# Graph network on one Trainium2 core: the edge keys and weight parts of strips 2 to 24 turned by a DMA transpose through DRAM

## The chip, the cores and the metric

The kernel runs on 1 core of one Trainium2 chip. The metric is the device time of one execution in microseconds (us). The kernel before took 1860.86 us, the median of three runs (1860.08 to 1861.27).

The names used below: PE is the engine for matrix products, PEld its weight loads, DVE the vector engine, ACT the scalar engine, POOL the general engine, and SP the engine that here does nothing but issue DMAs. Each engine works through its own instructions in order and waits only on semaphores. "SPq" and "POOLq" are rows of the sequencer.

## The reference

Four graph layers act in turn on a table `x` of 6250 nodes with 128 features. Each one normalises `x`, gathers neighbours over the 206250 edges (which are sorted by `dst`), sums them per node and adds the result to `x`.

```python
h = jnp.maximum(_layernorm(x, axis=-1), 0.0)
msg = edge_weight[:, None] * h[src]                       # layer 0
neighbor = jax.ops.segment_sum(msg, dst, num_segments=6250)
out = neighbor @ W1.T + b1 + (h * neighbor) @ W2.T + b2
x = x + jax.nn.leaky_relu(out, negative_slope=0.2)
...
agg = jax.ops.segment_sum(h[src], dst, num_segments=6250)  # layer 1, then by degree, gelu, graph norm
...
summed = jax.ops.segment_sum(x_clique[min(dst, 3124)], src, num_segments=6250)  # layer 2, mean over edges
...
agg = jax.ops.segment_sum(m[src], dst, num_segments=6250)  # layer 3, GRU gates
```

No gather is done row by row. The kernel first builds, for every strip of 256 destination nodes, a dense matrix of edge counts (for layers 1 to 3) and a dense matrix of edge weights (for layer 0), and the sums over edges become dense products.

## The kernel before

`fast` has two stages. In the first, which ends at about 1018 us of the profile, 25 strips are worked through one after another. `strip(k, nb)` covers 2 blocks of 128 nodes (the last strip one block). In the second stage, layers 1 to 3 run as dense products over the counts (`dense`, L1088) to the end. The change lies in the first stage alone.

**A strip.** It takes 8 pieces, and a piece 4 calls of `count`. A call makes 24 small products on PE (L781) of one-hot matrices, `s_hot` for the low 7 bits of the source and `k_hot` for its block, the latter times 1 and times three bf16 parts of the weight. ACT takes the result out of PSUM in two copies per call (L788 into `edge_w`, L790 into `cnt`). After every second call, `next(before)` issues a share of layer 0 of the strip before (L818, pairs of products that use one half of the array each). The one-hot matrices are made on DVE by `one_hots`, three instructions a piece (L759, L761, L762), one piece ahead: the pool `hot` has two buffers of each, so the matrices for piece p+1 can be written only when PE has finished piece p-1. The matrices for piece 0 of the next strip are made at the start of piece 7, from `following`, the pair of tiles that `prepare` hands out.

**What one-hots are made from.** `prepare(k)` is a generator that runs a strip ahead. It finds where the edges of 128 node pairs (one in each partition) begin, fetches 64 edges for each of the two nodes from the sorted lists with indirect DMAs on POOL (`fetch`, L639: `dst`, `src` and `wgt` for each half), and computes `vals`, five bf16 matrices of 128 pairs by 128 edges: two keys (L727, L730, on DVE) and three parts of the weight (`split`, L584 to L587, on POOL). The one-hots need these with edges along the partitions. So the last step turns them: five transposes on PE into one PSUM tile `pv` (L736), of the pool that the counts take their three buffers from too, and two copies on ACT into `keys` and `by_edge` (L741).

**The order.** It is written out by hand (`manual_schedule`), so an engine's instructions stand in the order in which Python issues them. `strip` calls `next(edges)` once at the middle of each piece named in `EDGES_AT` (in strip 0 at the start of the pieces in `FIRST_AT`), and a new `prepare(k + 2)` is begun at the end of piece 6 (`NEXT_AT`; in strip 0 after the last of `FIRST_AT`). In strips from 1 on the five steps are:

| step | piece | what `prepare` issues |
|---|---|---|
| begin | end of 6 | `junk` (L670, 1.9 us on DVE), fetch of `line` |
| 1 | 0 | `off` of half 0, fetch of `dst` half 0 |
| 2 | 2 | `off` of half 1, fetches `dst` half 1, `src` and `wgt` half 0 |
| 3 | 3 | fetches `src` and `wgt` half 1 |
| 4 | 5 | `vals`: keys on DVE, parts on POOL |
| 5 | 6 | five PE transposes, two ACT copies |

**What else the SP queue carries in a strip.** Two stores of finished counts (`cnt_d`, L969, 800 KB each, at the ends of pieces 3 and 7). Up to six steps of `turn` (`TURN_AT`: ends of pieces 1, 2, 3, 5, 6, 7), each a DMA transpose of 128 by 640 two-byte counts (`tt`, L801) and a store of the one before (L803); the 125 of them are through at about 895 us. From `finish0`, which ends the strip before, come a load of `xs` (piece 0), stores of `h_d` and `u_d` (L866, L867, piece 4) and a store of `f_d` (L880, piece 7). The add for `u_d` (L865) is on POOL.

Of the kernel before, what the change touches and what calls it, by code (L numbers as in the profile page):

```python
# [11 lines left out]
BF16 = mybir.dt.bfloat16  # L12
# [4 lines left out]
P = 128  # L17
# [454 lines left out]
TI = 2  # L472
# [22 lines left out]
U8, U16 = mybir.dt.uint8, mybir.dt.uint16  # L495
# [4 lines left out]
def fast(ctx: ExitStack, tc: tile.TileContext, a: dict, out: bass.AP, flag: bass.AP):  # L500


    nc = tc.nc
    const = ctx.enter_context(tc.tile_pool(name="f_const", bufs=1))
    dram = ctx.enter_context(tc.tile_pool(name="f_dram", bufs=1, space=bass.MemoryType.DRAM))
# [4 lines left out]
    identh = const.tile([P, P], BF16, name="f_identh")  # L510
# [23 lines left out]
    f_d = dram.tile([P, NB, D], F32, name="f_d")  # L534
    h_d = dram.tile([P, NB, D], F32, name="h_d")
    x_d = dram.tile([P, NB, D], F32, name="x_d")
    smp_d = dram.tile([NSMP, 1], I32, name="smp_d")

    def rows(table, g, nb):
# [42 lines left out]
    def split(eng, parts, src, rest):  # L582

        eng.tensor_copy(parts[0], src)  # L584
        eng.tensor_tensor(rest, src, parts[0], op=ALU.subtract)
        eng.tensor_copy(parts[1], rest)
        eng.tensor_tensor(parts[2], rest, parts[1], op=ALU.subtract)  # L587
# [9 lines left out]
    with ExitStack() as bx:  # L597
        def pool(name, bufs):
            return bx.enter_context(tc.tile_pool(name="b_" + name, bufs=bufs))
# [4 lines left out]
        banks = bx.enter_context(tc.tile_pool(name="b_banks", bufs=3, space=bass.MemoryType.PSUM))  # L604
# [28 lines left out]
        pay, hot = pool("pay", 2), pool("hot", 2)  # L633
# [4 lines left out]
        def fetch(t, name, idx):  # L638
            nc.gpsimd.indirect_dma_start(out=t, out_offset=None, in_=col[name],  # L639
                                         in_offset=bass.IndirectOffsetOnAxis(ap=idx, axis=0))  # L640
# [23 lines left out]
        def prepare(k):  # L664

            n0 = node0[:, k : k + 1]
            if k:
                junk = once.tile([P, NSMP], BF16, name="junk")
                r = small.tile([P, 1], F32, name="r")
                nc.vector.tensor_scalar(junk, smp, n0, None, op0=ALU.is_lt, op1=ALU.add, accum_out=r)  # L670
                at = small.tile([P, 1], F32, name="at")
                nc.vector.tensor_scalar(at, r, 1.0, 0.0, op0=ALU.subtract, op1=ALU.max)
                nc.vector.tensor_scalar(at, at, float(P), float(E - P), op0=ALU.mult, op1=ALU.min)
                at_i = small.tile([P, 1], I32, name="at_i")
                nc.vector.tensor_copy(at_i, at)  # L675
                line = once.tile([P, P], I32, name="line")
                fetch(line, "dst", at_i)
                yield
                less = once.tile([P, P], BF16, name="less")
                nc.vector.tensor_scalar(less, line, n0, None, op0=ALU.is_lt)  # L680
                c = small.tile([P, 1], F32, name="c")
                nc.vector.tensor_reduce(c, less, axis=mybir.AxisListType.X, op=ALU.add)
                off = small.tile([P, 1], F32, name="off")
                nc.vector.tensor_add(off, at, c)
            else:
                off = first_offsets()

            dst = once.tile([P, P], I32, name="dst")
            src = once.tile([P, P], I32, name="src")
            wgt = once.tile([P, P], F32, name="wgt")  # L690
            vals = pay.tile([P, 5, P], BF16, name="vals")
            same = once.tile([P, P], BF16, name="same")
            other = once.tile([P, P], BF16, name="other")
            halves_of = [(h, slice(h * H, (h + 1) * H)) for h in range(WN)]
            offs, nodes = [], []
            for h, half in halves_of:
                off_i = small.tile([P, 1], I32, name="off_i")
                nc.vector.tensor_scalar(off_i, off, float(E - H), None, op0=ALU.min)
                fetch(dst[:, half], "dst", off_i)
                offs.append(off_i)  # L700
                node = small.tile([P, 1], F32, name="node")
                nc.vector.tensor_scalar(node, n0, float(h), None, op0=ALU.add)  # L702
                nodes.append(node)
                if h + 1 == WN:
                    break
                if not k:
                    fetch(src[:, half], "src", off_i)
                    fetch(wgt[:, half], "edge_weight", off_i)
                yield
                here = deg[:, k, h : h + 1]  # L710
                nc.vector.tensor_scalar(same[:, half], dst[:, half], node, None, op0=ALU.is_equal,
                                        op1=ALU.add, accum_out=here)
                nc.vector.tensor_add(off, off, here)
            for (h, half), off_i in list(zip(halves_of, offs))[0 if k else 1 :]:
                fetch(src[:, half], "src", off_i)
                fetch(wgt[:, half], "edge_weight", off_i)
                yield
            one = nc.vector.tensor_scalar(same[:, half], dst[:, half], node, None, op0=ALU.is_equal,
                                          op1=ALU.add, accum_out=deg[:, k, WN - 1 : WN])
            if not k:  # L720
                first_same.append(one)
            for (h, half), node in zip(halves_of, nodes):
                nc.vector.tensor_scalar(other[:, half], dst[:, half], node, float(2 * P),
                                        op0=ALU.not_equal, op1=ALU.mult)
            sb = once.tile([P, P], I32, name="sb")
            nc.vector.tensor_scalar(sb, src, 7, None, op0=ALU.arith_shift_right)
            nc.vector.tensor_tensor(vals[:, 1, :], other, sb, op=ALU.add)  # L727
            sl = once.tile([P, P], I32, name="sl")
            nc.vector.tensor_scalar(sl, src, P - 1, None, op0=ALU.bitwise_and)
            nc.vector.tensor_copy(vals[:, 0, :], sl)  # L730
            rest = once.tile([P, P], F32, name="rest")
            split(nc.gpsimd, [vals[:, i, :] for i in (2, 3, 4)], wgt, rest)
            yield
            pv = banks.tile([P, 5, P], BF16, name="pv", tag="pK")
            for i in range(5):
                nc.tensor.transpose(pv[:, i, :], vals[:, i, :], identh)  # L736
            keys = pay.tile([P, P // TI, 2, TI], BF16, name="keys")
            parts = pay.tile([P, P // TI, 3, TI], BF16, name="by_edge")
            for t, i in ((keys, 0), (parts, 2)):
                to = pv[:, i : i + t.shape[2], :].rearrange("p i (q t) -> p q i t", t=TI)  # L740
                nc.scalar.copy(t, to)  # L741
            by_edge = keys, parts
            yield by_edge

        tq = TW // TI
# [148 lines left out]
        def normed(n):  # L894
            for _ in range(2 * n):
                next(norming)

        first = prepare(0)
        next(first)
        normed(4)  # L900
# [25 lines left out]
        by_edge = next(first)  # L926
        next(norming)
        hots = one_hots(by_edge, 0)
        before, ends, turns, edges = iter(()), [], turn(), prepare(1)


        END_AT, EDGES_AT, NEXT_AT = (0, 1, 2, 3, 4, 5, 7), (0, 2, 3, 5, 6), 6
        NORMS_AT = (0, 1, 3, 5), (0, 1, 2, 3)
        FIRST_AT = (2, 3, 4, 5, 6, 7)
        LAST_AT = (0, 2, 4, 6, 7, 10, 13)
        TURN_AT = (1, 2, 3, 5, 6, 7)

        def strip(k, nb):
# [4 lines left out]
            for w0 in range(0, last, PW):  # L943
                if w0 % TW == 0:
                    if k < 2 and piece in NORMS_AT[k]:
                        next(norming, None)
                    if not k and piece in FIRST_AT:
                        following = next(edges, None)
# [21 lines left out]
                if w1 % (PW * PT) and w1 < last:  # L970
                    continue
                if piece == (NEXT_AT if k else FIRST_AT[-1]) and k + 2 < NS:
                    edges = prepare(k + 2)
                    next(edges)
# [553 lines left out]
def gnn_kernel(tc: tile.TileContext, a: dict, out: bass.AP):  # L1528
    nc = tc.nc
    with tc.tile_pool(name="flag", bufs=1) as keep:  # L1530
        flag = keep.tile([1, 1], I32, name="flag")
        fast(tc, a, out, flag)
        found = nc.values_load(flag[0:1, 0:1], min_val=0, max_val=2 * E,
                               skip_runtime_bounds_check_because="a count of edges, each at most twice")
        with tc.If(found != E):
            general(tc, a, out)
# [48 lines left out]
```

## Time and profile before

| quantity | value |
|---|---|
| median of three runs | 1860.86 us |
| the profiled execution, as timed | 1859.0 us |
| its span, first to last instruction | 1857.2 us |
| first count of strip 0, on PE | 24.7 us |
| strip 0, from its first count to the next strip's | 41.4 us |
| strip 1 | 46.6 us |
| strips 2 to 23, together | 859.1 us |
| the shortest strip among them (23) | 38.63 us |
| the longest among them (3) | 41.60 us |
| first count of strip 24 | 971.7 us |

The lengths of strips are the distances between the first L781 product of one strip and of the next in the timeline. How to read the profile's lines: the page's first part gives each engine's busy time and share of the span. The 40 slices show busy tenths over time; one slice is 46.4 us, so the first stage is the first 22 slices. In a group of instructions, "a<-b" says which tile is written from which. "busy" counts overlapping instructions once. "mean" is the duration of one; on PE, where products overlap, it is far more than the distance from one to the next. A number in square brackets in a timeline is the idle time of that engine just before, with what ended it; "issue" there means that the profile shows nothing that was waited for.

Where the engines stand in the first stage, from the groups of instructions:

```profile
L741 ACT COPY by_edge<-pv 128x384 bf16<-128x384 bf16 x25 | 12.2, 490 | 0.0
L741 ACT COPY keys<-pv 128x256 bf16<-128x256 bf16 x25 | 9.4, 377 | 16.4 <-PE pv L736 16.4
L736 PE MATMUL pv<-f_identh,vals 128*128 128x128 bf16 x125 | 12.4, 227 | 14.6 <-DVE vals L730 12.5 <-POOL vals L584 1.3 <-POOL vals L586 0.6
```

These are the instructions that the change touches: 25 groups of five transposes and 25 pairs of copies. Of the 14.6 us that PE waited, 12.5 are one wait, at the very start of the kernel.

### The profile page before, as it was taken

The page shows a single profiled execution, that of the slowest core. Times are in us where ns is not written, and L with a number is a line of the kernel's source. Part 1 is how long each engine was busy: PE and PEld are TensorE (multiplying, and loading weights), DVE is VectorE, ACT ScalarE, POOL GpSimd, SP SyncE. Part 2 cuts the span into 40 slices and gives each one's busy share as a digit, 9 for nine tenths or more (in the row PEclk, how much of TensorE's full clock was granted, in tenths as well). Part 3 has the DMA queues.
Part 4 walks back from the last instruction along what each step waited for, and adds up shares of the span by engine and source line. Part 5 has one row for each costly group of instructions (what it writes and reads, how often), then busy time and mean ns, then how long its engine had stood idle before and what let it go on. Part 6 is the DMA issues. An engine that isn't in the chain of part 4 may idle for free. (4 is left out here: it accounts for less than half of the span.)

```text
span 1857.2 us, 65339 instructions
## 1 busy us (share of the span) xinstructions
PE 1791.2 (96%) x28191; PEld 1521.2 (82%) x28191; DVE 1381.6 (74%) x2946; ACT 1208.7 (65%) x2835; POOL 471.6 (25%) x431
## 2 busy tenths in 40 slices
PE   2799999999999999999999999999999999999997
PEld 2688888888888888888888888888888877787776
DVE  7878888888888888888886777777787755454444
ACT  6777777777777777777774677777565654443443
POOL 2333333433334333334332111111122210000000
PEclk9899999999999999999999999999999999999999
DMA  4245454644644544545223555554555444344342
GB/s 106 58 123 115 101 139 106 129 126 100 136 106 118 122 103 126 117 99 132 72 79 117 179 173 162 167 154 124 143 155 147 139 148 142 121 136 148 121 140 60
DMA packets 262513, 231.72 MB, mean 125 GB/s; under 512 B 101518, under 2 KB 246424, under 8 KB 262215
## 3 DMA queue, kind: packets, MB, share of 16 engines
q1 hardware_dynamic: 253415, 210.67, 42.4%
q0 software_dynamic: 8800, 16.78, 3.2%
q8 instruction: 223, 3.65, 0.8%
q14 instruction: 75, 0.61, 0.1%
HBM read 130.37 MB, written 76.54 MB: 111 GB/s over the span
## 5 line engine op out<-in xcount | busy, mean ns | idle before, releaser
L818 PE MATMUL pM<-edge_w,h 64*128 64x256 f32 (+1 forms) x2450 | 619.2, 387 | 0.2
L818 PE MATMUL pB<-edge_w,h 64*128 64x256 f32 (+1 forms) x2450 | 617.8, 387 | 0.7 <-ACT agg L826 0.3
L1088 PE MATMUL acc<-wide,parts 128*128 128x512 f32 (+2 forms) x2548 | 574.3, 383 | 2.7 <-DVE wide L1066 1.3
L1088 PEld LDWEIGHTS acc<-wide,parts 128*128 128x128 f32 x2548 | 460.0, 188 | 101.2 <-issue 10.5
L790 ACT CAST cnt<-pK 128x400 uint8<-128x400 f32 x784 | 394.9, 504 | 222.5 <-PE pK L781 187.4
L781 PEld LDWEIGHTS <-s_hot 64*128 64x128 bf16 x18816 | 382.9, 95 | 80.5 <-issue 21.5
L818 PEld LDWEIGHTS pB<-edge_w,h 64*128 64x128 f32 x2450 | 421.6, 187 | 31.5 <-issue 3.3
L781 PE MATMUL pK<-k_hot,s_hot 64*128 64x49 bf16 (+1 forms) x18816 | 404.5, 192 | 32.2 <-DVE k_hot L762 19.2
L818 PEld LDWEIGHTS pM<-edge_w,h 64*128 64x128 f32 x2450 | 421.6, 187 | 5.4 <-issue 2.9
L788 ACT COPY edge_w<-pK 128x392 f32<-128x392 f32 x784 | 397.0, 506 | 0.0
L759 DVE TENSOR_TENSOR s_hot<-iota,keys 128x2048 bf16<-128x2048 bf16 x196 | 240.7, 1228 | 85.5 <-remote 52.5
L762 DVE TENSOR_TENSOR k_hot<-k_hot,by_edge 128x2352 bf16<-128x2352 bf16 x196 | 271.6, 1386 | 8.4
L1066 DVE TENSOR_SCALAR_CACHE_REDUCE wide<-ring 128x512 fp32r<-128x512 uint8 (+2 forms) x325 | 193.4, 651 | 25.3 <-issue 15.6
L1064 ACT ACTIVATE wide<-ring 128x512 fp32r<-128x512 uint8 (+2 forms) x312 | 184.7, 595 | 24.3 <-ACT wide L1064 19.6
L639 POOL DMA_INDIRECT dst<-in_dst,off_i x50 | 84.1, 1682 | 360.7 <-DVE node L702 341.6
L1058 ACT CAST wide<-ring 128x1024 fp32r<-128x1024 uint8 (+3 forms) x130 | 120.7, 957 | 70.6 <-PE acc L1088 65.7
L1057 DVE CAST wide<-ring 128x1536 fp32r<-128x1536 uint8 (+2 forms) x130 | 119.6, 945 | 53.4 <-PE acc L1088 41.5
L1088 PE MATMUL acc<-wide,q_parts 128*128 128x512 f32 (+2 forms) x650 | 157.3, 392 | 1.2 <-DVE wide L1043 0.9
L1088 PEld LDWEIGHTS acc<-wide,q_parts 128*128 128x128 f32 x650 | 115.6, 188 | 28.5 <-DVE wide L1043 3.1
L761 DVE TENSOR_TENSOR k_hot<-iota,keys 128x800 bf16<-128x800 bf16 x196 | 112.4, 573 | 0.0
L1429 POOL DMA_DIRECT2D out<-x x12 | 10.2, 853 | 322.9 <-DVE x L1426 293.1
L639 POOL DMA_INDIRECT line<-in_dst,at_i x24 | 40.9, 1703 | 163.2 <-DVE at_i L675 155.3
(246 smaller groups left out, 1650.3 us busy)
## 6 DMA issues: line engine op xcount, KB each, us to landing
ring<-cnt_d SPq DMA_DIRECT2D x110, 640.0 KB
cnt_d<-cnt SPq DMA_DIRECT2D x49, 800.0 KB
cntT_d<-tt SPq DMA_DIRECT2D x125, 160.0 KB
ring<-cntT_d SPq DMA_DIRECT2D x60, 320.0 KB
ring<-cnt_d SPq DMA_DIRECT2D x10, 480.0 KB
ring<-cnt_d SPq DMA_DIRECT2D x10, 320.0 KB
h<-in_x SPq DMA_DIRECT2D x12, 256.0 KB
xs<-in_x SPq DMA_DIRECT2D x24, 128.0 KB
```

Of the source, the lines that this page charges most:

```text
L639: nc.gpsimd.indirect_dma_start(out=t, out_offset=None, in_=col[name], in_offset=bass.IndirectOffsetOnAxis(ap=idx, axis=0))
L759: nc.vector.tensor_tensor(s_hot, count_up(P), at(0, P), op=ALU.is_equal)
L762: nc.vector.tensor_tensor(k_hot[:, :, 1:, :NB], k_hot[:, :, :1, :NB].to_broadcast([P, tq, 3, NB, TI]), parts.to_broadcast([P, tq, 3, NB, T ...
L781: nc.tensor.matmul(pk[:, h, to], s_hot[r, u, :, t], rhs, start=j == 0, stop=True, skip_group_check=True)
L788: nc.scalar.copy(m.rearrange("p b (i h) -> p b i h", h=WN), by_block[:, 1, :NB])
L790: nc.scalar.copy(m.rearrange("p b e (i h) -> p b e i h", h=WN), by_block[:, 0].rearrange("p (b e) i h -> p b e i h", e=2))
L818: nc.tensor.matmul(pl[h][:, :w], h0[r, s, :], edge_w[r, s, :w], start=s == 0, stop=s == NB - 1)
L1057: nc.vector.tensor_copy(*(v[:, :3].rearrange("p k b n -> p b k n") for v in (to, of)))
L1058: nc.scalar.copy(to[:, 3:ks], of[:, 3:ks])
L1064: one = nc.scalar.activation(to[:, k], of[:, k], AF.Copy, accum_out=total)
L1066: one = nc.vector.tensor_scalar(to[:, k], of[:, k], 1.0, None, op0=ALU.mult, op1=ALU.add, accum_out=total)
L1088: nc.tensor.matmul(acc[:, : nb * P], parts[:, s, j, :], rhs, start=s + j == 0, stop=s == end and j == 1)
```

## The change

It has three parts. A DRAM tile `vals_d` with two slots is added. In `prepare` for k of 2 and more, four SP stores (even and odd node pairs, keys and parts) put `vals` there, already in the row order that the one-hots want, and in the next step one DMA transpose on SP brings the 640 rows of 128 back as `turned_vals`; the five PE transposes and two ACT copies stay for strips 0 and 1 alone. `keys` and `by_edge` become two views of one tile.

The fetches of `src` and `wgt` for half 0 are issued at once after that of `dst` half 0 (before, this was so for k = 0 alone), and those of half 1 after `dst` half 1. That takes one step out of the generator, so `EDGES_AT` goes from (0, 2, 3, 5, 6) to (0, 2, 4, 5), and `FIRST_AT` loses its 7. The steps now: piece 0, three fetches; piece 2, three fetches; piece 4, `vals` and the four stores; piece 5, the transpose. In strip 0 the steps up to the PE transposes end at piece 6, and `prepare(2)` begins at the end of piece 6 in place of piece 7.

```diff
+    vals_d = dram.tile([2, 5 * P, P], U16, name="vals_d")
...
-                if not k:
-                    fetch(src[:, half], "src", off_i)
-                    fetch(wgt[:, half], "edge_weight", off_i)
+                fetch(src[:, half], "src", off_i)
+                fetch(wgt[:, half], "edge_weight", off_i)
                 yield
...
-            for (h, half), off_i in list(zip(halves_of, offs))[0 if k else 1 :]:
+            for (h, half), off_i in list(zip(halves_of, offs))[1:]:
                 fetch(src[:, half], "src", off_i)
                 fetch(wgt[:, half], "edge_weight", off_i)
                 yield
...
             split(nc.gpsimd, [vals[:, i, :] for i in (2, 3, 4)], wgt, rest)
+            if k > 1:
+                for i, n in ((0, 2), (2, 3)):
+                    to = vals_d[k % 2, i * P : (i + n) * P, :].rearrange("(q i t) e -> t q i e", i=n, t=TI)
+                    for t in range(TI):
+                        nc.sync.dma_start(to[t], vals[t::TI, i : i + n, :].bitcast(U16))
             yield
-            pv = banks.tile([P, 5, P], BF16, name="pv", tag="pK")
-            for i in range(5):
-                nc.tensor.transpose(pv[:, i, :], vals[:, i, :], identh)
-            keys = pay.tile([P, P // TI, 2, TI], BF16, name="keys")
-            parts = pay.tile([P, P // TI, 3, TI], BF16, name="by_edge")
-            for t, i in ((keys, 0), (parts, 2)):
-                to = pv[:, i : i + t.shape[2], :].rearrange("p i (q t) -> p q i t", t=TI)
-                nc.scalar.copy(t, to)
-            by_edge = keys, parts
+            turned_vals = pay.tile([P, 5 * P], BF16, name="by_edge")
+            by_edge = [turned_vals[:, i * P : (i + n) * P].rearrange("p (q i t) -> p q i t", i=n, t=TI)
+                       for i, n in ((0, 2), (2, 3))]
+            if k < 2:
+                pv = banks.tile([P, 5, P], BF16, name="pv", tag="pK")
+                for i in range(5):
+                    nc.tensor.transpose(pv[:, i, :], vals[:, i, :], identh)
+                for t, i in zip(by_edge, (0, 2)):
+                    nc.scalar.copy(t, pv[:, i : i + t.shape[2], :].rearrange("p i (q t) -> p q i t", t=TI))
+            else:
+                nc.sync.dma_start_transpose(turned_vals.bitcast(U16), vals_d[k % 2])
             yield by_edge
...
-        END_AT, EDGES_AT, NEXT_AT = (0, 1, 2, 3, 4, 5, 7), (0, 2, 3, 5, 6), 6
+        END_AT, EDGES_AT, NEXT_AT = (0, 1, 2, 3, 4, 5, 7), (0, 2, 4, 5), 6
...
-        FIRST_AT = (2, 3, 4, 5, 6, 7)
+        FIRST_AT = (2, 3, 4, 5, 6)
```

## The prediction

> **What bounds the kernel now.** I read the page's busy line and slices first, then the stage in question cut at the five PE transposes of each strip, then the timelines of PE, POOL, DVE and SP inside one strip.
>
> ```profile
> PE 1791.2 (96%) x28191; PEld 1521.2 (82%) x28191; DVE 1381.6 (74%) x2946; ACT 1208.7 (65%) x2835; POOL 471.6 (25%) x431
> 613.30:652.50 39.20, 39.11 (x993) 34.28 (x991) 32.55 (x61) 29.16 (x71) 13.69 (x12) 1.00 0.51 116
> 886.60:925.20 38.60, 38.44 (x992) 34.22 (x990) 33.09 (x60) 28.85 (x71) 14.52 (x12) 1.00 0.21 71
> ```
>
> The second and third lines are two strips: length, then busy time of PE, PEld, DVE, ACT, POOL, then clock and DMA share. PE is busy throughout, DVE for 33 of 38.6 us, ACT for 29. So strips 2 to 23 are PE's. Comparing, for each piece, the end of its last k_hot (L762) with PE's first product on it, DVE is ahead by 0.6 (piece 1) to 1.9 us, never late after strip 3. What leaves PE's queue is therefore worth its full distance, until DVE's smallest lead is used up.
>
> **The PE transposes, removed 23 times (k = 2 to 24).** PE's timeline at two seams between layer-0 products and a count, one without and one with transposes:
>
> ```profile
> 961.15 0.38 PE L818 MATMUL pM<-edge_w,h 64*128 64x256 f32 x1
> 961.35 0.95 PE L781 MATMUL pK<-k_hot,s_hot 64*128 64x99 bf16 x47
> ...
> 963.33 0.38 PE L818 MATMUL pM<-edge_w,h 64*128 64x256 f32 x1
> 963.64 0.45 PE L736 MATMUL pv<-f_identh,vals 128*128 128x128 bf16 x5
> 964.02 0.97 PE L781 MATMUL pK<-k_hot,s_hot 64*128 64x99 bf16 x48
> ```
>
> From start to start it is 0.20 us without and 0.69 with: 0.49 for a group. The 0.69 is the same at all 23. 23 x 0.49 = 11.3 us. The instruction's own duration (219 ns, so 25.2 us for 115) is pipelined and is no price here. The Trainium skill (TensorE: Matmul & The Clock Gate, Part 4: PE-mode transpose) gives about 275 ns for such a transpose within a kernel; by it the sum would be an estimated 31.6 us, but the seam shows 0.49 for five, and the seam decides. The two ACT copies (0.86 us a strip) lie under ACT's 10 us of idle time a strip: nothing.
>
> Does DVE leave room for it? In strip 11 the vals work on DVE (491.74 to 493.69, 1.95 us) stood between the matrices of pieces 6 and 7. It moves to piece 4, where DVE waits for PE's buffer:
>
> ```profile
> 488.58 1.33 DVE L759 TENSOR_TENSOR s_hot<-iota,keys 128x2048 bf16<-128x2048 bf16 x1 [2.59 <-remote]
> ...
> 499.04 1.23 DVE L759 TENSOR_TENSOR s_hot<-iota,keys 128x2048 bf16<-128x2048 bf16 x1
> ```
>
> 1.95 us fit in 2.59. The lead at pieces 7, 0 and 1, the smallest (1.0, 1.05, 0.61), is then about as it was or better, even with PE 0.49 earlier.
>
> **The round trip through DRAM.** Added per strip: four SP stores of 128 or 192 rows of 256 B, one DMA transpose. Neither a store of 256 B rows nor a load of this shape is in the trace; the nearest rows are the stores of `f_d`, `u_d` and `cntT_d` (issue 0.32 to 0.56 us; from issue to the last completion mark 1.7 to 5.1, u_d's median 2.4) and the `tt` transposes, which move the same 160 KB (issue 1.2 to 2.7, landed 2.7 to 6.6 after their start, median 4.1).
>
> ```profile
> 487.13 0.95 POOL L639 DMA_INDIRECT wgt<-in_edge_weight,off_i  x1 [0.30 <-issue]
> ...
> 488.86 0.32 SPq L867 DMA_DIRECT2D u_d<-xs  x1
> 489.23 1.21 SPq L801 DMA_TRANSPOSE tt<-cnt_d  x1
> 490.49 0.56 SPq L803 DMA_DIRECT2D cntT_d<-tt  x1
> 491.10 2.05 SPq L801 DMA_TRANSPOSE tt<-cnt_d  x1
> 493.81 0.32 SPq L803 DMA_DIRECT2D cntT_d<-tt  x1
> ```
>
> In strip 11's times: the last wgt fetch moves to about 483.0 (the second of today's five-fetch run), the split on POOL starts 3.7 later (median over the strips, as today) and not before L865's add, now near 487: 487.5, and takes 2.5 (1.7 to 4.0): 490.0. Two stores: 490.9; landed 2.4 later: 493.3. The transpose waits for that on SP, then 4.1: 497.4. DVE wants it at 498.8 (piece 7's matrices start at 493.1, when PE leaves piece 5, 3.2 us; then `junk` and its followers, 2.5), and PE is 1.0 behind DVE. It is in time by 1.4, by 2.4 for PE: nothing on the path. Ends: with the fastest store and transpose (1.7 and 2.7) 3.5 in time; with the slowest (split 4.0, store 5.1, transpose 6.6) 5.2 + 1.5 = 6.7 later than reckoned, 4.3 late for PE, which 23 times would be 99 us.
>
> The Trainium skill (DMA: Bandwidth & Descriptors, Specifications) speaks against rows of 256 B: it puts line rate at 512 B and more, with a read-modify-write below. By a doubled store time, an estimate, 2.4 us would be gone and with it the slack; no row of this trace shows that.
>
> What stands behind on SP: during the wait the two `turn` steps above (489.23 to 494.13, 4.9 us) stand behind the transpose, and now begin near 495 and end near 500. Next on SP is f_d, whose data came at 502.6 in this strip: 2.6 us spare. A `cnt` store delayed by that is used a block of 19 us later. Nothing.
>
> **The fetches, regrouped: PE's starved stretches.** Strips 2 to 23 take 859.1 us, but 22 times the undisturbed 38.63 is 849.9. The missing 9.2 us are gaps on PE marked "issue":
>
> ```profile
> 603.85 0.22 PE L781 MATMUL pK<-k_hot,s_hot 64*128 64x49 bf16 x3 [0.38 <-issue]
> 604.59 0.18 PE L781 MATMUL pK<-k_hot,s_hot 64*128 64x49 bf16 x1 [0.52 <-issue]
> ...
> 595.89 1.74 POOL L639 DMA_INDIRECT dst<-in_dst,off_i  x1 [7.22 <-DVE node L702]
> 602.02 1.61 POOL L639 DMA_INDIRECT src<-in_src,off_i  x1 [0.31 <-issue]
> 603.94 0.95 POOL L639 DMA_INDIRECT wgt<-in_edge_weight,off_i  x1 [0.30 <-issue]
> ```
>
> Every such gap lies late in a run of five fetches on POOL (9.0 us long), never near a single one. At the same place the 16 KB packets of the instruction queue, normally 4.9 us apart, are at 599.88 and 606.63. In strip 1 the run (83.67 to 90.16) has no 16 KB packet between 82.38 and 92.00, PE falls into steps of 0.74 us for 4.5 us, and the granted clock falls after it. I read it as instructions that come late while POOL's fetches are dealt out. Runs of three are 5.4 us; in strips 2 to 23 only two stretches of gaps began earlier than 7.4 us into a run. But strips 22 and 23, after the last `tt`, hold almost none, so DMA transposes have a part in it too, and a seventh is added to six. Bounds: all 9.2 gone, or one sixth more (+1.5). I take half: -4.6.
>
> **Strips 0 and 1.** In strip 0 DVE sets the pace (its lead is 0.06 us at pieces 1 to 5). `vals` of strip 1 moves to piece 5, where src half 1, now the fifth of six fetches in a row on POOL, lands some 2 us later than DVE asks, and PE's transposes then stand before piece 6. But a wait of 2.75 us on DVE for the ACT copies at the strip's end goes, and `junk` (2.5 us) comes out of strip 1. I reckon strip 1's second piece 1 us later; ends 0 to +3. In strip 1 the run of fetches ends some 2.5 us earlier, which takes as much out of the starved 4.5: I take -2, ends -6 (with the clock's loss) and 0.
>
> **Sum** against the profiled span: -11.3 - 4.6 + 1 - 2 = -16.9, 1857.2 to 1840.3. That execution was timed at 1859.0, the median of the runs is 1.9 above it; 1860.9 - 16.9 = 1844.
>
> **Rivals.**
>
> *Only the transposes count.* The gaps stay, because the transposes and the cnt stores cause them rather than the length of a run: -11.3 and the early strips' -1 to +1: 1849.5. For it: strips 22 and 23 have runs of five and next to no gaps. Against: strip 1 starves with no SP DMA between 72 and 92 us.
>
> *The gaps grow.* More DMA at the busiest time makes them twice what they were: +9.2 - 11.3 = -2: 1859. For it the same two strips; against, that the new packets come after the fetches and the cnt store, not with them.
>
> *The round trip is late (slower).* Place: the wait of s_hot at piece 7 for `turned_vals`. It decides once the transpose lands 2.4 us later than reckoned; with POOL's split at 4.0 and store and transpose each 1.2 us above my rows it is 3.9 later, PE stands 1.5 us in each of 23 strips, 34.5 - 11.3 = +23: 1884. For it: the chain has four links of which three show tails of 2 us. Against: nothing else is on SP's queue at that time.
>
> *It does not do what it says*: PE keeps waiting for something else at that seam, so that 0.49 is not all freed. DVE's lead speaks against it; it would end near 1856.
>
> **How the numbers follow.** Forecast 1844 (1838 to 1848): 0.48. Only the transposes: 0.27. Gaps grow, or little freed: 0.12, of which half within 0.2%. Round trip late: 0.13, nearly all slower. A measurement of this kernel can tell 0.2%, 3.7 us, from no change. Faster by over that 0.81, within it 0.07, slower 0.12. The range reaches from 1836 (all gaps and 1 us of the early strips' gain: -11.3 - 9.2 - 4 = -24.5) up to 1860, where the first two rivals end; what is left out is mostly the late round trip. Forecast and first rival alone: 1838 to 1852.
>
> **What would show it.** Piece 6 of a strip, 4.87 us from count to count, becomes 4.38; PE transposes into `pv` are 10 in place of 125. DVE s_hot at the first piece of a strip shows no wait for the DMA of `by_edge`. "issue" gaps on PE in strips 2 to 23 fall below 9.2 us. SP's f_d store comes no later against PE. A wait of s_hot for a DMA of over 1 us, once in each strip, would make the prediction wrong; so would strips longer than 38.2 us with gaps elsewhere.

## The result, and the profile after

The changed kernel is slower: a median of 1877.73 us over 7 runs (1868.53 to 1888.63) against 1861.32 over 7 runs of the kernel before. The ratio is 1.0089, its 95% interval 1.0068 to 1.0109. The forecast was 1844, the range 1836 to 1860. Of the rivals, "The round trip is late" (1884) is the one that came about. The profiled execution took 1879.46 us, with a span of 1878.0.

The spans, cut as before at the first count of each strip (L788 in the changed kernel):

| stage, us | before | after |
|---|---|---|
| first count of strip 0 | 24.7 | 24.5 |
| strip 0 | 41.4 | 45.1 |
| strip 1 | 46.6 | 40.1 |
| strips 2 to 23 | 859.1 | 883.8 |
| the shortest among them | 38.63 | 38.23 |
| what follows | 885.5 | 884.5 |
| span | 1857.2 | 1878.0 |

The loss is in strips 2 to 23, +24.7 us. The page's busy line of the changed kernel, and below it two rows of its view of the waits (who waited for whom: us in total, times, longest):

```profile
PE 1785.4 (95%) x28076; PEld 1541.3 (82%) x28076; DVE 1392.4 (74%) x2946; ACT 1193.3 (64%) x2789; POOL 483.2 (26%) x431
```

```profile
DVE s_hot L766 <- DMA by_edge<-vals_d: 50.9, 13, 6.9
...
PE pK L788 <- DVE fs L885: 26.5, 11, 4.9
```

PE has 115 instructions fewer, the 23 groups of five transposes, and is busy for 5.8 us less. But a new wait is there: 13 times DVE's first matrices of a strip wait for the tile that the DMA engines turn, 50.9 us in all. Before, these matrices never waited for a DMA. PE's share of it is named after `fs`, because the count takes a PSUM buffer (`pK`) that DVE's `fs` (L885) has to read out first, and `fs` stands on DVE behind the late matrices: 26.5 us, 11 times.

One such strip in order of time: the turned tile of strip 12, made during strip 11 (start, duration, engine, line, operation; in brackets the idle time before it and what ended it).

```profile
487.19 1.86 POOL L640 DMA_INDIRECT wgt<-in_edge_weight,off_i  x1 [0.30 <-issue]
487.52 0.34 SPq L976 DMA_DIRECT2D cnt_d<-cnt  x1
...
490.92 0.84 POOL L872 TENSOR_TENSOR xs<-xs,h 128x256 f32<-128x256 f32 x1 [1.87 <-ACT h L580]
...
494.05 1.25 POOL L585 CAST vals<-wgt 128x128 bf16<-128x128 f32 x1 [2.28 <-DMA wgt<-in_edge_weight,off_i]
495.38 1.51 POOL L586 TENSOR_TENSOR rest<-wgt,vals 128x128 f32<-128x128 f32 x1
496.95 0.52 POOL L587 CAST vals<-rest 128x128 bf16<-128x128 f32 x1
497.55 1.48 POOL L588 TENSOR_TENSOR vals<-rest,vals 128x128 bf16<-128x128 f32 x1
...
502.94 1.17 SPq L749 DMA_TRANSPOSE by_edge<-vals_d  x1
...
507.99 1.22 DVE L766 TENSOR_TENSOR s_hot<-iota,by_edge 128x2048 bf16<-128x2048 bf16 x1 [6.87 <-DMA by_edge<-vals_d]
...
511.03 0.42 DVE L885 TENSOR_TENSOR fs<-pf,f_bl 128x256 f32<-128x256 f32 x1
...
511.50 0.91 PE L788 MATMUL pK<-k_hot,s_hot 64*128 64x99 bf16 x29 [4.87 <-DVE fs L885]
```

The first two rows are the ones that matter. The last weight fetch of the strip starts 0.33 us ahead of the store of the counts, 800 KB. It lands at 493.93 by its completion marks, 6.74 us after its start; the split (L585) waits for it to the end, takes 4.98 us in place of the 2.5 that I took, and what follows is late by that. DVE stands for 6.87 us, PE for 4.87.

PE's waits are not the whole price. Stretches of the changed kernel (bounds; then length, and busy us of PE, PEld, DVE, ACT, POOL; then the granted clock, DMA share and GB/s): an undisturbed strip, strip 11 with the wait at its end, strip 12, the first piece of strip 12, and the first piece of strip 13.

```profile
188.27:226.50 38.23, 38.08 (x986) 34.13 (x983) 33.67 (x60) 28.43 (x69) 14.90 (x12) 1.00 0.48 124
468.37:511.50 43.13, 38.11 (x986) 35.05 (x983) 33.61 (x61) 28.78 (x70) 16.11 (x12) 1.00 0.46 111
511.50:551.96 40.46, 39.95 (x984) 36.69 (x985) 33.68 (x60) 27.96 (x68) 13.70 (x12) 0.96 0.52 123
511.50:517.55 6.05, 6.05 (x124) 5.53 (x125) 5.13 (x11) 3.22 (x8) 0.37 (x1) 0.72 0.93 245
551.97:556.65 4.68, 4.68 (x127) 4.56 (x125) 4.01 (x7) 3.53 (x9) 0.00 (x0) 1.00 1.08 210
```

After the wait the first piece takes 6.05 us at a granted clock of 0.72, in place of 4.68 at 1.00. In strips 2 to 23 there are six such episodes of clock 0.5, of 3.4 or 6.8 us, 27.3 us together, each at a wait of PE of 2.2 us or more; before there was none in these strips. The first pieces of those six strips are 9.8 us longer together than 4.68 each. So the +24.7 us of strips 2 to 23 are: 22 x -0.49 = -10.8 for the transposes, +26.5 for the waits, and +9.0 left over, close to the 9.8 of the first pieces at the lowered clock.

**Who is late, and who is not.** I followed the chain of each of the 23 tiles through the completion marks. Two kinds of strips stand apart:

| in the changed kernel | 14 tiles | 9 tiles |
|---|---|---|
| count store starts after the weight fetch by | 0.03 to 0.37 us | 1.8 to 4.0 us |
| weight fetch lands after its start | 4.9 to 6.9 | 2.4 to 4.3 |
| split takes, median | 4.2 | 2.8 |
| turned tile lands after the start of the fetch, median | 17.8 | 15.1 |
| PE's wait before the strip's first count, sum | 26.3 | 0.25 |

In all 14 the fetch's last completion mark comes after the store's last; in the 9, the fetch has landed before the store's data are through. Eight of the 9 were made in a strip that began with a wait of PE of 1.6 us or more: there the distance between fetch and store is the larger one.

Not every late tile costs PE something. In four of the 14, whose splits took 2.45 to 3.76 us, PE did not wait; in the ten others the split took 3.6 to 5.2. And in eight of the 9 the split did not wait for the fetch either: it started 5.3 to 6.1 us after the fetch, right behind POOL's `xs` add (L872), which waits for ACT.

The packets that the trace records on the DMA engines show what the late fetch waits for. A weight fetch is 64 packets in two halves of 32. In the strip above the first half is through 0.84 us after the start of the fetch. From 488.30 to 491.25 the DMA engines carry 608 packets of SP's queue, which fill their time (share 100.6%), and none of the fetch. The last packet of the 800 KB ends 3.75 us after the start of the fetch, and the second half begins at 4.14. In the 14 tiles the last data packet starts 3.7 to 6.2 us after the fetch does, in the 9 it starts at 1.8 to 2.1, once at 3.2. So the data were late, not only the completion marks.

There is a rival in the same rows: the fetch's own instruction on POOL took 1.83 to 1.90 us in 13 of the 14, and 0.94 to 1.11 in the 9, and with no store in the way the second half starts 0.7 us after that instruction's end. That is 1 us at most. The runs below part the two: in the changed kernel again (e6) and in e4, which moves the store, the instruction takes the same 1.5 us (median), but the second half starts at 3.2 to 6.0 us in 22 of 23 tiles of e6, and at 1.8 to 2.2 in all 23 of e4.

### The profile page after: what moved, and what is told of

Its sections match the earlier page's. It is cut to its first block, busy times and chain, and to the rows that moved or that the text cites. A ratio compares the mean times of both kernels' runs of the same rounds, so it can differ in the third digit from the quotient of the medians.

```text
span 1878.0 us, 65213 instructions
## 1 busy us (share of the span) xinstructions
PE 1785.4 (95%) x28076; PEld 1541.3 (82%) x28076; DVE 1392.4 (74%) x2946; ACT 1193.3 (64%) x2789; POOL 483.2 (26%) x431
## 3 DMA queue, kind: packets, MB, share of 16 engines
q1 hardware_dynamic: 285063, 218.22, 44.7%
## 5 line engine op out<-in xcount | busy, mean ns | idle before, releaser
L788 PEld LDWEIGHTS <-s_hot 64*128 64x128 bf16 x18816 | 396.0, 95 | 95.5 <-issue 33.0
L788 PE MATMUL pK<-k_hot,s_hot 64*128 64x49 bf16 (+1 forms) x18816 | 408.8, 193 | 54.3 <-DVE fs L885 26.5
L766 DVE TENSOR_TENSOR s_hot<-iota,by_edge 128x2048 bf16<-128x2048 bf16 x196 | 239.9, 1224 | 96.6 <-DMA by_edge<-vals_d 50.9
L768 DVE TENSOR_TENSOR k_hot<-iota,by_edge 128x800 bf16<-128x800 bf16 x196 | 116.5, 595 | 0.0
L640 POOL DMA_INDIRECT src<-in_src,off_i x50 | 77.1, 1542 | 15.2 <-issue 15.2
```

Of the source, the lines that this page charges most:

```text
L766: nc.vector.tensor_tensor(s_hot, count_up(P), at(0, P), op=ALU.is_equal)
L788: nc.tensor.matmul(pk[:, h, to], s_hot[r, u, :, t], rhs, start=j == 0, stop=True, skip_group_check=True)
```

## The experiments

The theory after these lines: the round trip costs time only because its first link, the last weight fetch, was moved to a place 0.3 us ahead of the count store, and lands after it. The rivals: the added DMA traffic itself disturbs the kernel; the regrouped fetches do; the chain is too long wherever it starts.

The record names chip 1 for e1 to e4 and chip 15 for e5 to e8, and no chip for the comparison above, which I call the first chip. The kernel before takes 1839.13 us on chip 1 (21 runs) and 1838.37 on chip 15 (13 runs), in place of 1861.32. So each ratio is to the kernel before on the same chip. The kernel before was profiled on chip 15 alone (e5), so the stages of e1 to e4 are held against a profile of another chip. The stages:

| kernel | median, us | ratio and interval | strip 0 | strip 1 | strips 2-23 | PE waits for `fs`, us (times) | clock 0.5 in strips 2-23, us |
|---|---|---|---|---|---|---|---|
| before (e5, chip 15) | 1839.44, one run | - | 41.1 | 40.1 | 846.4 | 0 | 0 |
| changed (e6, chip 15) | 1845.47 | 1.0043, 1.0026 to 1.006 | 43.8 | 37.1 | 849.3 | 16.5 (11) | 3.4 |
| e1 (chip 1) | 1837.27 | 0.9992, 0.9982 to 1.0001 | 43.3 | 38.8 | 843.6 | 0 | 0 |
| e2 (chip 1) | 1911.0 | 1.0373, 1.0335 to 1.041 | 41.8 | 42.8 | 918.9 | 59.9 (22) | 64.9 |
| e3 (chip 1) | 1835.95 | 0.9982, 0.9973 to 0.9992 | 44.3 | 37.8 | 844.5 | 0 | 0 |
| e4 (chip 1) | 1824.32 | 0.992, 0.9907 to 0.9934 | 42.8 | 37.1 | 831.8 | 1.6 (3) | 0 |
| e7 (chip 15) | 1821.66 | 0.9908, 0.9891 to 0.9924 | 44.7 | 37.1 | 830.5 | 0 | 0 |
| e8 (chip 15) | 1841.48 | 1.002, 1.0011 to 1.003 | 44.8 | 37.1 | 850.7 | 0.5 (1) | 0 |

**e1, the regrouped fetches alone.** The fetches and steps of the changed kernel, but PE transposes in every strip, in piece 6, and no round trip.

```diff
-            if k > 1:
+            if False:
                 for i, n in ((0, 2), (2, 3)):
...
-            if k < 2:
+            if True:
                 pv = banks.tile([P, 5, P], BF16, name="pv", tag="pK")
...
-        END_AT, EDGES_AT, NEXT_AT = (0, 1, 2, 3, 4, 5, 7), (0, 2, 4, 5), 6
+        END_AT, EDGES_AT, NEXT_AT = (0, 1, 2, 3, 4, 5, 7), (0, 2, 4, 6), 6
```

> The regrouped fetches alone: all five matrices are transposed on PE again, in piece 6; nothing goes through DRAM. Theory (the round trip comes late): the 26.6 us of PE waits before a strip's first count and the 9 us of lowered clock and remainder go, the 11.3 us of PE transposes come back, strips 0 and 1 keep their 2.8 us: 1857 to 1863 us. Rival (the regrouping itself costs, by fetches that collide with the count stores or by instructions that come late): 1868 us or more. My forecast of 4.6 us less of gaps marked issue would be seen here too: 6.2 us of them before, 6.1 after the change, so I now expect 5 to 7.

Measured: ratio 0.9992, not to be told from no change. Gaps of "issue" on PE in strips 2 to 23 are 0.7 us (2 times), against 2.2 (4 times) in the kernel before on chip 15 (e5). So regrouping is not the loss, and here there was little for it to gain.

**e2, the round trip alone.** The fetches and steps of the kernel before, with the round trip behind them (the diff is to the changed kernel; against the kernel before only the round trip is new).

```diff
-                fetch(src[:, half], "src", off_i)
-                fetch(wgt[:, half], "edge_weight", off_i)
+                if not k:
+                    fetch(src[:, half], "src", off_i)
+                    fetch(wgt[:, half], "edge_weight", off_i)
...
-            for (h, half), off_i in list(zip(halves_of, offs))[1:]:
+            for (h, half), off_i in list(zip(halves_of, offs))[0 if k else 1 :]:
...
-        END_AT, EDGES_AT, NEXT_AT = (0, 1, 2, 3, 4, 5, 7), (0, 2, 4, 5), 6
+        END_AT, EDGES_AT, NEXT_AT = (0, 1, 2, 3, 4, 5, 7), (0, 2, 3, 5, 6), 6
...
-        FIRST_AT = (2, 3, 4, 5, 6)
+        FIRST_AT = (2, 3, 4, 5, 6, 7)
```

> The round trip through DRAM with the steps of before: fetches in five, vals in piece 5, the DMA transpose in piece 6. Theory (late round trip): the chain starts one piece later than in the changed kernel but its last fetch no longer stands just ahead of the count store, so a shorter lateness in nearly every strip: s_hot waits for by_edge in at least 15 of 23 strips, 0.5 to 3 us for PE each; 1862 to 1900 us. Rival (it is the DMA load, not the wait): strips lose time without a wait of s_hot for by_edge.

Measured: 3.7% slower, more than the 2% expected at most. Its view of the waits:

```profile
DVE s_hot L767 <- DMA by_edge<-vals_d: 78.1, 20, 5.7
...
PE pK L789 <- DVE fs L886: 59.9, 22, 4.1
```

Nearly every strip waits now, since the chain begins later; the fetch itself is quick here (3 to 5 us). This shows what the regrouping is for, that the place of the wait is the one named, and that the time at the lowered clock grows with the waits: 64.9 us at 0.5. A late fetch is thus not the only way for the tile to come late.

**e3, the traffic without the wait.** e1 with the four stores and the DMA transpose of the changed kernel, at their places; the transpose fills a spare tile that nobody reads, and the one-hots use PE's.

```diff
-            if False:
+            if k > 1:
...
+            if k > 1:
+                spare = pay.tile([P, 5 * P], BF16, name="spare")
+                nc.sync.dma_start_transpose(spare.bitcast(U16), vals_d[k % 2])
+                yield
...
-        END_AT, EDGES_AT, NEXT_AT = (0, 1, 2, 3, 4, 5, 7), (0, 2, 4, 6), 6
+        END_AT, EDGES_AT, NEXT_AT = (0, 1, 2, 3, 4, 5, 7), (0, 2, 4, 5, 6), 6
```

> As the regrouped kernel with PE transposes, and besides it the four stores and the DMA transpose of each strip, into a tile that nobody reads. Theory (late round trip): the traffic costs nothing by itself, the same time as the regrouped fetches alone within 3 us: 1857 to 1866. Rival (DMA load, late instructions): most of the 16 us that the change lost are here: 1870 or more.

Measured: 0.9982, against 0.9992 for e1. The transfers, their issues on SP and what stands behind them there cost nothing that can be seen. The rival "traffic" falls.

**e4, the count store out of the way.** The changed kernel, with the store of a strip's first block of counts held back from the end of piece 3 to the end of piece 5, behind the transpose.

```diff
-                    nc.sync.dma_start(cnt_d[c, :, i, :], flat(cnt))
+                    done = cnt_d[c, :, i, :], flat(cnt)
+                    if k and w1 < last:
+                        held = done
+                    else:
+                        nc.sync.dma_start(*done)
...
+                if held and piece == 5:
+                    nc.sync.dma_start(*held)
```

> The changed kernel, with the store of the first block of counts issued after the DMA transpose (end of piece 5) in place of the end of piece 3, so that the last weight fetch no longer has 800 KB close behind it on the DMA engines. Theory (late round trip, begun by the late weights): the weights land 2.5 to 3.5 us after the fetch starts in place of 5 to 7 in the late strips, the transposed tile lands 13 to 15.5 us after it in place of 17 to 21, waits of s_hot for by_edge all but vanish, the clock stays up: 1842 to 1850 us. Rival (the tail lies in POOL's split, stores or transpose rather than in the weights): 1860 or more with waits still there.

Measured: 0.992, faster than the kernel before. Rows of its views of the waits, and POOL's timeline in one strip:

```profile
DVE s_hot L766 <- DMA by_edge<-vals_d: 23.6, 14, 2.6
...
PE pK L788 <- DVE fs L885: 1.6, 3, 0.8
```

```profile
501.06 1.48 POOL L640 DMA_INDIRECT wgt<-in_edge_weight,off_i  x1 [0.30 <-issue]
504.82 0.73 POOL L872 TENSOR_TENSOR xs<-xs,h 128x256 f32<-128x256 f32 x1 [2.29 <-ACT h L580]
505.50 0.29 POOL L585 CAST vals<-wgt 128x128 bf16<-128x128 f32 x1
```

The weight fetch now lands in 2.5 to 4.9 us (median 3.0), and the split starts a median of 4.5 us after it. I expected DVE's waits for the tile to all but vanish; they are still 23.6 us, in 14 strips, but the longest is 2.6 us, and PE waits 1.6 us in all. Ten of the 22 strips are 37.72 to 37.73 us, 0.48 below the undisturbed 38.21 of the kernel before on chip 15, and the clock is not lowered in any. Moving one store, with every part of the change in place, turns +0.4% (e6) into -0.8%. The store's place on SP's own queue is not what matters: in the strip of the changed kernel above, SP had reached the stores of `vals` at 492.16, 1.9 us before the split began.

**e5 and e6, both kernels again.** No edit: the kernel before and the changed kernel as they are, for their profiles on this chip.

> The kernel before, for its profile beside the others of this chip: strips 2 to 23 without disturbance, 38.2 us each if the chip is the one of the first four runs; gaps marked issue on PE near 6 us, as on the other chip (with runs of three fetches they were 0.6 and 1.3 there), or near 1 if that is the chip's doing.

> The changed kernel as it is. Theory (late round trip): 1.004 to 1.012 of the kernel before, late strips where the last weight fetch starts 0.3 us before the count store, with PE waits of 20 us or more and the clock lowered after the long ones.

Measured: the undisturbed strip of the kernel before is 38.21 us here, 38.63 on the first chip, and its gaps of "issue" are 2.2 us. Two rows of the changed kernel's view of the waits:

```profile
DVE s_hot L766 <- DMA by_edge<-vals_d: 43.2, 16, 5.7
...
PE pK L788 <- DVE fs L885: 16.5, 11, 3.7
```

The changed kernel loses 0.4% here and 0.9% on the first chip: 22 of its 23 weight fetches land late here, at 4.4 to 6.8 us, but the rest of the chain is shorter (the split takes a median of 3.6 us), and PE's waits add up to 16.5 us, where I expected 20 or more. So the sign and the place are the same on both chips; the size is not.

**e7, the split ahead of POOL's add.** In e4 the split waited for POOL's `xs` add (L872), which stood ahead of it on POOL and waited for ACT. e7 is e4 with the step of `prepare` issued ahead of that of `end` in piece 4.

```diff
                 if w0 // PW % PT == PT // 2:
+                    if k and piece in EDGES_AT and piece == 4:
+                        following = next(edges, None)
                     if piece in END_AT:
                         next(end, None)
...
-                    if k and piece in EDGES_AT:
+                    if k and piece in EDGES_AT and piece != 4:
                         following = next(edges, None)
```

> The kernel with the count store after the transpose, and besides it the edges' step of piece 4 issued ahead of the end of the strip before, so that POOL's split does not stand behind the add L872. The split then starts 3 us after the last weight fetch in place of 4.45, the transposed tile lands some 1.4 us earlier, waits of s_hot for by_edge fall from 23.6 us to under 10. PE lost only 1.6 us to them, so the time is that of the kernel with the late count store within 3 us: 0.990 to 0.993 of the kernel before. If it is the load on the DMA engines that sets the landing, the waits stay.

Measured: 0.9908. Against e4 the time is not told apart (the intervals overlap), but the waits are. A row of its view of the waits, and the timelines of SP and POOL in a strip of e7:

```profile
DVE s_hot L766 <- DMA by_edge<-vals_d: 3.9, 6, 2.1
```

```profile
502.29 1.50 POOL L640 DMA_INDIRECT wgt<-in_edge_weight,off_i  x1 [0.30 <-issue]
505.42 0.29 POOL L585 CAST vals<-wgt 128x128 bf16<-128x128 f32 x1 [1.63 <-issue]
...
506.39 3.19 SPq L737 DMA_DIRECT2D vals_d<-vals  x4
...
508.33 1.87 POOL L872 TENSOR_TENSOR xs<-xs,h 128x256 f32<-128x256 f32 x1
...
511.11 1.58 SPq L749 DMA_TRANSPOSE by_edge<-vals_d  x1
512.75 0.57 SPq L989 DMA_DIRECT2D cnt_d<-cnt  x1
```

The split starts 3.1 us after the fetch, in place of 4.4 in the strip of e4 and 6.9 in that of the changed kernel, the store of the counts goes behind the transpose, and 3.9 us are left of the wait for the tile, none of which reaches PE: its strips 2 to 23 take 830.5 us, 22 x 37.73 = 830.1. This is the best version found, 0.9% below the kernel before.

**e8, another fetch in the bad place.** The changed kernel with the last two fetches of the second run exchanged, so that `src` and not `wgt` stands ahead of the count store, which stays where it was.

```diff
             for (h, half), off_i in list(zip(halves_of, offs))[1:]:
-                fetch(src[:, half], "src", off_i)
                 fetch(wgt[:, half], "edge_weight", off_i)
+                fetch(src[:, half], "src", off_i)
```

> The changed kernel with the last two fetches of a strip exchanged: dst, weights, src. Theory (the fetch just ahead of the count store is the one that lands late, whichever it is): the weights land 2.5 to 4 us after their start, src 5 to 7; waits of s_hot for by_edge shrink by more than half, and DVE waits at L726 for src instead, 1 to 4 us in each of these strips: 0.995 to 1.008 of the kernel before. Rival (the weights are late because of their own size or place on POOL): they stay late.

Measured: 1.002. The weights land in 2.8 to 4.5 us, and now `src` lands in 4.6 to 6.9 (22 of the 23 tiles). Its view of the waits and the timelines of POOL, SP and DVE in one strip:

```profile
DVE sb L726 <- DMA src<-in_src,off_i: 69.1, 24, 3.8
```

```profile
471.36 1.60 POOL L640 DMA_INDIRECT wgt<-in_edge_weight,off_i  x1 [0.30 <-issue]
473.27 1.49 POOL L640 DMA_INDIRECT src<-in_src,off_i  x1 [0.30 <-issue]
473.55 0.34 SPq L976 DMA_DIRECT2D cnt_d<-cnt  x1
...
477.70 0.29 POOL L585 CAST vals<-wgt 128x128 bf16<-128x128 f32 x1
478.07 0.43 POOL L586 TENSOR_TENSOR rest<-wgt,vals 128x128 f32<-128x128 f32 x1
478.56 0.29 POOL L587 CAST vals<-rest 128x128 bf16<-128x128 f32 x1
478.93 0.43 POOL L588 TENSOR_TENSOR vals<-rest,vals 128x128 bf16<-128x128 f32 x1
...
479.85 0.23 DVE L726 TENSOR_SCALAR sb<-src 128x128 int32<-128x128 int32 x1 [3.48 <-DMA src<-in_src,off_i]
```

The wait goes to whoever needs the fetch that stands just ahead of the store: it was 1.2 us for `src` in e6 and is 69.1 here. The wait for the tile falls from 43.2 to 5.3 us, but DVE, held up at `sb`, is late with its next matrices, and PE waits 13.9 us for them in strips 2 to 23 (18 times). With DVE idle beside it the split takes 1.67 us; that second finding is taken up below.

## Why the prediction was wrong, step by step

**The step that failed: the first two links of "The round trip through DRAM".** It said: "the last wgt fetch moves to about 483.0 (the second of today's five-fetch run), the split on POOL starts 3.7 later (median over the strips, as today)". The 3.7 is the time from fetch to split at the old place, where the fetch starts 3.7 us behind the count store. At the new place the split started a median of 6.6 us after the fetch in the 14 late tiles, and of 5.5 in the others, right behind POOL's add. And the row for the new place stood in the trace of before, two lines of POOL's and SP's timelines that I had not put side by side:

```profile
483.02 1.89 POOL L639 DMA_INDIRECT wgt<-in_edge_weight,off_i  x1 [0.31 <-issue]
```

```profile
483.39 0.34 SPq L969 DMA_DIRECT2D cnt_d<-cnt  x1
```

This fetch, of the first half, landed 6.82 us after its start by its completion marks. In the kernel before, 21 of the 23 first-half weight fetches stand 0.35 to 0.39 us ahead of the store; they land in 4.0 to 7.1 us, median 5.8, in all 21 after the store's last mark. There nobody needed them so early, so no wait showed it. With 5.8 in place of the 4.5 that I had from fetch to split (483.0 to 487.5), 1.3 of the 2.4 us of reserve are gone at the median, and all of it, by 2.6, at 7.1. The Trainium skill (DMA: Bandwidth & Descriptors, Queues, rings and completion order) says that a DMA's completion increment lands only after every earlier write of the same DMA engine, across its queues. The order of the marks in the 14 and 21 cases agrees with that. But the packets show that the larger part of the delay is in the data: in the 14 tiles the last data packet started at 3.7 to 6.2 us, the last mark came 0.6 to 2.4 us behind it, in the other 9 by 0.4 to 1.0.

**"Takes 2.5 (1.7 to 4.0)".** Second mis-sized term: 4.98 in strip 11, a median of 4.2 in the late tiles, up to 5.2. At the new place the split lies beside DVE's one-hots: in strip 11 the four instructions take 1.25, 1.51, 0.52 and 1.48 us, in e8, where DVE was idle, 0.29, 0.43, 0.29 and 0.43. Strip 11 of the changed kernel, by my own links from the start of the fetch: to the split 4.5 reckoned, 6.85 measured; split 2.5, 4.98; stores landed 3.3, 3.84; transpose 4.1, 5.03 with the pause before it. Together 14.4 and 20.7: 6.3 late, of which 4.8 are these two links. The reserve was smaller than reckoned, too. DVE had done its other work 32.75 us after the strip's first count, not at 34.3 (498.8), since PE was done with the matrices of piece 5 earlier; and for PE the tile could have come 1.9 us after the reckoned time, not 2.4. The tile was 6.7 us late (0.3 of it because the fetch itself started later in the strip), and 6.7 less 1.9 gives 4.8, against the 4.87 that PE waited.

**The stores of 256 B rows and the DMA transpose** were sized about right: stores landed in 1.9 to 4.5 us, median 2.8 (2.4 taken), transposes in 2.5 to 5.2, median 3.4 (4.1 taken). What stands behind them on SP cost nothing (e3), as said.

**The PE transposes** were right: piece 6 was to go from 4.87 to 4.38 us and went to 4.34 to 4.36; with the waits gone the strip is 0.48 shorter (38.21 to 37.73). The cover on ACT and DVE held.

**The "issue" gaps, -4.6**, failed where I had read them: on that chip the gaps marked so are 5.1 us (14 times) before and 4.7 (13 times) after. So of the 9.2 us that I called such gaps only 5.1 are marked, and one of the 14, 0.24 us at 157.18, does stand beside a single fetch. More lies below the gaps that are marked: on the first chip piece 5 of the kernel before, which begins as its run of five fetches ends, took 0.3 to 0.5 us more than on chip 15 in most strips (5.01 us in strip 4, against 4.48). In the changed kernel piece 5 of strip 4 is 4.48, but piece 2, which begins as its first run of three ends, went from 4.35 to 4.69. So far as these pieces show, the stretch moved with the fetches rather than went. On chip 15 the same kernel before had 2.2 us of gaps, on chip 1 e1 had 0.7. Why the chips differ stays open.

**Strips 0 and 1** were taken as +1 and -2; they are +3.7 and -6.5 on the first chip, +2.7 and -3.0 on chip 15.

**The rival** "The round trip is late" had place and direction right. That its 1884 is near the 1878 is luck: it reckoned 34.5 us of standing, 1.5 in each of 23 strips, from a slow split, store and transpose; 26.5 were measured, in 11 strips, and 9.0 of lowered clock and remainder, which it did not name, made up the rest. A slow split is among its conditions, a late fetch is not. Its "Against: nothing else is on SP's queue at that time" looked at the wrong thing. The store was not ahead on SP's queue; it was beside the fetch on the DMA engines. With that undone, and the split ahead of the add, the forecast's sum comes out, but by luck, not term by term: -16.9 were forecast, and e7's ratio of 0.9908 is -16.9 of 1838.4. Of its profile's -16.9 us (1837.6 to 1820.7), -15.9 are in strips 2 to 23 (10.6 by the 0.48 of each strip, the rest stalls that the kernel before has on this chip), +3.6 in strip 0, -3.0 in strip 1 and -1.6 behind strip 23.

## What to carry to other kernels

When a transfer is moved, price it by a transfer that already stands at the new place, not by its own duration at the old one, and look for large transfers that start within half a microsecond of it, on any queue. A chain that was hidden needs its reserve counted with the tails of all links, since it is PE that pays, twice: for the wait and for the clock after it. If such a chain is late, move the large transfer that nobody waits for before giving up the change.

## What the runs showed of the hardware

The landing of a fetch of some 2.5 us became 5 to 7 us when an 800 KB store started 0.3 us behind it on another queue; with 1.8 us or more between them it was 2.4 to 4.3. The fetch goes in two halves, and its second half came behind the store's packets: in the strip above at 4.14 us, in place of 1.65.

In strips 2 to 24, waits of PE of 2.1 to 4.9 us before a strip's first count went with a granted clock of 0.5 for 3.4 or 6.8 us, which began between 2.5 us before the end of the wait and 1.2 us after it. Over the changed kernel, e2 and e6 this was so for all 18 waits of 2.7 us or more, for 3 of the 11 of 2.1 to 2.6, and for none of 1.9 or less. It is no rule for the whole kernel: the wait of 3.8 us before the first count of strip 0 had no such episode. The Trainium skill (TensorE: Matmul & The Clock Gate, Why this matters for your kernels) puts the limit at idle gaps of about 3 us; here gaps from 2.1 us on could be enough.

The same kernel took 1861 us in one set of runs and 1838 to 1839 on chips 1 and 15, 1.2% less, and the places where PE starves differ with it.
